# Fewer GpSimd operations for a threshold search's first points, an empty step behind them, and one scratch row for two tiles

## The chip, the cores and the metric

The kernel runs on one core of a Trainium2 chip. The core has five engines that run their own instruction queues and meet through semaphores: TensorE (PE in the profile; PEld is its weight load), VectorE (DVE), ScalarE (ACT), GpSimd (POOL) and SyncE (SP), which here only starts DMAs. The metric is the device time of one launch in microseconds; the median of several runs is compared.

## The reference

Layer 0 is a graph-attention layer over a 2708 x 2708 adjacency matrix. Layer 1 is what the change is about. It takes `X` (2708 x 512) and makes two diffusion stages:

```python
for s in range(STEPS):                       # STEPS = 2
    A = _adj_from_feats(Xa, W1, W2, W3)
    Xf = Rf @ Xf
    Xb = Rb @ Xb
    Xa = A @ Xa
    Z = Z + (Xf @ U1[s] + Xb @ U2[s] + Xa @ U3[s])
```

`_adj_from_feats` forms logits `Q W2 K^T` and takes, in every row, the smallest set of largest softmax weights that reaches 0.9 of the row's mass; the softmax is then formed over that set alone. `Rf` and `Rb` are the adjacency matrix plus identity, divided by its row sums or column sums.

## The kernel before

**Tiles and stages.** The 2708 rows are 22 tiles of 128 (the last has 20). Layer 1 works on pairs of tiles, 11 groups in each of two stages (`s` = 0 and 1). For a group, TensorE makes the logits into `p` (L517), ScalarE copies them to SBUF (L519) and takes the exponential (L549, L556), VectorE searches the threshold of each row and writes the kept weights into two rows `keep[0]` and `keep[1]`, TensorE transposes these (L1004) and multiplies them with the values `va` (L1023), and the results are mixed with the matrices `U` (L1051). The products of the adjacency matrix (L959) run between these.

**Pipelining of groups.** In one turn of the loop (index `g`), TensorE works on group `g` with kept rows found earlier, VectorE searches group `g + 1`, and ScalarE and GpSimd prepare group `g + 2`: `Logits.exp` gives a list of small steps that the attention of group `g` takes up one after the other. The list holds, for each tile, `root` (the exponential at half scale; its sum is `half`) and `full` (the exponential itself; its sum is `tot`), then `points`, then twelve looks (a Relu and a Sign pass over 2708 elements for each of three points and two tiles), then `masses`. `points` is GpSimd work: from `tot` and `half` it guesses a threshold, makes three points around it (`ABOUT`), and writes their fourth powers and the negatives `nth`, which are the biases of the looks. `masses` combines what the looks counted; the search of that group begins from it.

**Order.** TensorE, ScalarE, VectorE and SyncE run under `tc.manual_schedule`: their instructions are queued in the order in which the program states them. GpSimd's order is chosen by the framework's planner. `paced(steps, n)` takes the next `n` steps from a list. In `attended` there are twelve turns `n` (six column groups for each of two tiles): each transposes the rows for the next turn (the copy to SBUF is ScalarE's L1008, tile `at`), takes steps from the list beginning at `n` = 3, and then multiplies. In stage 0 it takes two steps at `n` = 3 to 8 and one from 9 on; in stage 1 one at 3 to 5 and two from 6 on. `mixed` takes one step at each of up to six places (the first three of four row blocks of `U1` and of `U2`). `others` holds adjacency products and, in every second group of stage 0, eight steps `scaled`: ScalarE scales a finished product (L965, tile `xe`, two buffers), GpSimd stores it (L966), and VectorE splits it into two parts (L181, L182). These groups are called split groups below, and the other ones plain groups.

**Beginning of a stage.** At `g` = -1 the program takes `5 + G * NA` = 11 steps from the list of group 1 (four exponentials, `points`, six looks), and the rest at the top of the next turn, behind the logits of group 2: `paced(looks, len(looks))`.

**The search.** `search` makes interpolation rounds (L624 sums what lies above a threshold), then `late()` queues the attention of the group before, and then `finish` runs: for each tile it writes the elements below the threshold (L800) and takes the eight largest (`MAX8`, L802), once in stage 0 and twice in stage 1; then `kept_from` (L725) or `kept_ranked` (L730 to L733) writes the kept row of each tile. `keep` has two buffers, so the row that `finish` writes for tile `i` is the row of the group before that TensorE transposes. The four buffers of `p` hold two groups: the logits of group `g + 2` go where those of group `g` lay, once the search of group `g` has ended (L884 is the branch at its end).

Of the kernel before, what the change touches and what calls it, by code (L numbers as in the profile page):

```python
# [9 lines left out]
F32 = mybir.dt.float32  # L10
# [5 lines left out]
OP = mybir.AluOpType  # L16
# [8 lines left out]
P = 128  # L25
# [6 lines left out]
X_LO = math.exp(-4.0)  # L32
# [4 lines left out]
GUESS = ((0.715, -0.82, 0.4), (0.711, -0.798, 0.392))  # L37
ABOUT = (0.88, 1.0, 1.12)
# [15 lines left out]
def kernel(  # L54
# [19 lines left out]
    nc = tc.nc  # L74
# [3 lines left out]
    STEPS = u1.shape[0]  # L78
# [12 lines left out]
    G = 2  # L91
# [4 lines left out]
    const = ctx.enter_context(tc.tile_pool(name="const", bufs=1))  # L96
# [105 lines left out]
    with ExitStack() as l0:  # L202
# [13 lines left out]
        with tc.tile_pool(name="l0w", bufs=1) as wp, tc.tile_pool(name="l0p", bufs=2) as pp, \  # L216
# [44 lines left out]
            for t in range(NT):  # L261
                pr = rows[t]
# [52 lines left out]
        small = l0.enter_context(tc.tile_pool(name="l0small", bufs=3))  # L315
# [82 lines left out]
        for ci, tiles in enumerate(tchunks):  # L398
# [4 lines left out]
            for t in range(NT):  # L403
                pr = rows[t]
# [16 lines left out]
            for grp, r_b in zip(hgroups, r_bs):  # L421
                po = [ps_o.tile([P, 512], F32, name="po")[:DV] for _ in grp]
                for t in range(NT):
                    pr = rows[t]
# [29 lines left out]
    for r, c0, c1 in [(P, 0, NFULL), (rows[-1], NFULL, NT)]:  # L454
        if c0 == c1:
            continue
        s = (slice(0, r), slice(c0, c1))
# [11 lines left out]
    powers = const.tile([P, STEPS, 2, G], F32, name="powers")  # L469
    for s in range(STEPS):  # L470
        for i in range(2):
            nc.vector.memset(powers[:, s, i], GUESS[s][i])
    weights = const.tile([P, G + 1], F32, name="weights")
    for i in range(G + 1):
        nc.vector.memset(weights[:, i:i + 1], float(1 << i))
    NA = len(ABOUT)
# [11 lines left out]
    class Logits:  # L488
# [33 lines left out]
        def exp(self, looks=True):  # L522


            _, small, _ = self.pools
            gp = nc.gpsimd
            grp = self.grp
            self.tot = small.tile([P, G], F32, name="tot")
            self.half = small.tile([P, G], F32, name="half")

            self.pts = small.tile([P, NA, 3, G], F32, name="pts")
            self.th = small.tile([P, NA, G], F32, name="th_a")
            self.thr, self.top, self.cap = (small.tile([P, G], F32, name=n) for n in ("thr", "top", "cap"))
            self.nth = small.tile([P, NA, G], F32, name="nth", bufs=1)
            self.above = small.tile([P, NA, G], F32, name="above", bufs=1)
            self.signs = small.tile([P, NA, G], F32, name="signs", bufs=1)
            self.ragged = any(rows[t] < P for t in grp) or len(grp) < G
            if self.ragged:
                for x in (self.tot, self.half, self.above, self.signs, self.pts):
                    nc.gpsimd.memset(x, 1.0)  # L540
            nmx = small.tile([P, 2, G], F32, name="nmx1")
            for i, t in enumerate(self.grp):
                pr = rows[t]
                nc.vector.tensor_reduce(nmx[:pr, 0, i:i + 1], self.p[i][:pr], axis=AX.X, op=OP.max, negate=True)  # L544

            def over(i, func, **kw):
                pr = rows[self.grp[i]]
                junk = small.tile([P, N], U8, name="junk_a", bufs=1)
                nc.scalar.activation(junk[:pr], self.p[i][:pr], func, **kw)  # L549

            def root(i, pr):
                nc.scalar.mul(nmx[:pr, 1, i:i + 1], nmx[:pr, 0, i:i + 1], 0.5)
                over(i, AF.Exp, scale=0.5, bias=nmx[:pr, 1, i:i + 1], accum_out=self.half[:pr, i:i + 1])

            def full(i, pr):
                nc.scalar.activation(self.p[i][:pr], self.p[i][:pr], AF.Exp, bias=nmx[:pr, 0, i:i + 1],  # L556
                                     accum_out=self.tot[:pr, i:i + 1])

            def points():
                x0 = small.tile([P, 2, G], F32, name="x0")  # L560
                gp.tensor_tensor(x0[:, 0], self.tot, powers[:, self.s, 0], op=OP.pow)
                gp.tensor_tensor(x0[:, 1], self.half, powers[:, self.s, 1], op=OP.pow)
                gp.tensor_tensor(x0[:, 0], x0[:, 0], x0[:, 1], op=OP.mult)
                gp.tensor_scalar(x0[:, 0], x0[:, 0], math.exp(GUESS[self.s][2]), X_LO * 1.5, op0=OP.mult, op1=OP.max)
                for j, m in enumerate(ABOUT):
                    gp.tensor_scalar(self.pts[:, j, 0], x0[:, 0], m, 0.9995, op0=OP.mult, op1=OP.min)
                gp.tensor_tensor(self.th, self.pts[:, :, 0], self.pts[:, :, 0], op=OP.mult)
                gp.tensor_tensor(self.th, self.th, self.th, op=OP.mult)
                gp.tensor_scalar(self.nth, self.th, -1.0, None, op0=OP.mult)  # L569
                gp.tensor_scalar(self.thr, self.tot, P_NUC, None, op0=OP.mult)  # L570
                gp.tensor_scalar(self.top, self.tot, 1.0 + CURVE, None, op0=OP.mult)
                gp.tensor_scalar(self.cap, self.tot, CAP, None, op0=OP.mult)

            def masses():
                gp.tensor_scalar(self.signs, self.signs, 0.5, 0.5 * N, op0=OP.mult, op1=OP.add)
                gp.tensor_tensor(self.signs, self.signs, self.th, op=OP.mult)
                gp.tensor_tensor(self.pts[:, :, 2], self.signs, self.above, op=OP.add)

            steps = []
            for i, t in enumerate(self.grp):  # L580
                steps += [lambda a=(i, rows[t]): root(*a), lambda a=(i, rows[t]): full(*a)]
            steps.append(points)
            if looks:
                for i, t in enumerate(self.grp):
                    for j in range(NA):
                        for func, to in ((AF.Relu, self.above), (AF.Sign, self.signs)):
                            def look(i=i, j=j, pr=rows[t], func=func, to=to):
                                over(i, func, bias=self.nth[:pr, j, i:i + 1], accum_out=to[:pr, j, i:i + 1])
                            steps.append(look)
                steps.append(masses)  # L590
            return steps

    def search(lg, looked, early, late):
# [4 lines left out]
        v = nc.vector  # L598
# [4 lines left out]
        keep = [wide.tile([P, N], F32, name="keep") for _ in tiles]  # L603
# [189 lines left out]
        def finish(go):  # L793


            for i, pr in tiles:
                t, m = th[:pr, i:i + 1], kept[:pr, 1, i:i + 1]
                for e in range(0, nx, 8):
                    vs, ss = vn[:pr, i, e:e + 8], sn[:pr, i, e:e + 8]
                    v.scalar_tensor_tensor(keep[i][:pr], ps_[i][:pr], t, ps_[i][:pr], op0=OP.is_lt, op1=OP.mult,  # L800
                                           accum_out=left[:pr, i:i + 1] if e else None)
                    v.max(vs, keep[i][:pr])  # L802
                    if e:
                        m = left[:pr, i:i + 1]
                        v.tensor_tensor(m, tot[:pr, i:i + 1], m, op=OP.subtract)
                    v.tensor_tensor_scan(ss, vs, vs, m, OP.add, OP.bypass)
                    t = vn[:pr, i, e + 7:e + 8]
# [58 lines left out]
        def branch(go):  # L866
# [17 lines left out]
            for arm in tc.Switch({DVE: what}, (1 << G) + 1):  # L884
                if 0 < arm < 1 << G:
                    ties([x for x in tiles if arm >> x[0] & 1])
                elif arm == 1 << G and go == 0:
                    rounds(MORE_ROUNDS)
                    choose()
                    finish(1)  # L890
                elif arm == 1 << G and go == 1:
                    v.copy_predicated(th, short, vn[:, :, nx - 1])
                    v.copy_predicated(kept[:, 1], short, den)
                    finish(2)
                elif arm == 1 << G:
                    bisect()

        late()
        finish(0)
        rden = small.tile([P, G], F32, name="rden1")  # L900
        v.reciprocal(rden, den)
        return keep, rden

    for s in range(STEPS):
        last = s == STEPS - 1
        with ExitStack() as st:
# [6 lines left out]
            small = st.enter_context(tc.tile_pool(name=f"s{s}small", bufs=2))  # L913
# [225 lines left out]
            with tc.manual_schedule(engines={PE, ACT, DVE, SP}):  # L1139
# [4 lines left out]
                steps = lg[0].exp(looks=False)  # L1144
# [4 lines left out]
                half = []  # L1149
# [90 lines left out]
```

## Time and profile before

| What | us |
|---|---|
| Median of 3 runs | 3777.57 (3777.3 to 3778.19) |
| The profiled execution, its own time | 3774.21 |
| Its span from first to last instruction | 3772.1 |
| TensorE busy | 3383.3 (90%) |
| VectorE busy | 2611.1 (69%) |
| ScalarE busy | 1540.1 (41%) |
| GpSimd busy | 838.2 (22%) |
| Mean granted TensorE clock (share of full) | 0.956 |

Layer 0 takes the span up to about 1065 us; stage 0 runs from there to about 2340 us, stage 1 from there to the end. A row of the timeline gives the start, the duration, engine and line, operation, tiles written and read, their shapes, and in brackets how long the engine had been idle and what ended the idle time. A row of the waits gives who waited for whom, the total, the number of waits and the longest. A row of the windows gives the stretch, its length, then for each engine the busy time and (number of instructions), the granted clock, the DMA share and GB/s. Times are positions in the span.

### The profile page before, as it was taken

How to read it: one execution, taken by the hardware profiler on the slowest of the kernel's cores; microseconds unless marked ns; L12 is line 12 of the kernel's file. 1: busy time of each engine (PE TensorE's matmuls, PEld its weight loads, DVE VectorE, ACT ScalarE, POOL GpSimd, SP SyncE). 2: the span in 40 equal slices, each digit the busy share in tenths (PEclk: the TensorE clock that was granted, in tenths of full speed). 3: DMA queues.
4: the chain of work that ended last, by engine and by line, in shares of the span. 5: the costliest groups of instructions: out<-in, count | busy, mean ns of one | idle time of the engine just before them, and what ended most of it. 6: DMA issues, size and time to landing. Idle time of an engine off the chain costs nothing. (4 is left out here: it accounts for less than half of the span.)

```text
span 3772.1 us, 35425 instructions
## 1 busy us (share of the span) xinstructions
PE 3383.3 (90%) x11143; PEld 1760.6 (47%) x11143; DVE 2611.1 (69%) x4814; ACT 1540.1 (41%) x2334; POOL 838.2 (22%) x1187
## 2 busy tenths in 40 slices
PE   8999999999855898989898998668999999999988
PEld 4433333333533455545454453435555665556443
DVE  4588888989946526474554641967779798777992
ACT  2343202111025565546566621335544556445511
POOL 4115151423331121121212020302121211212101
PEclk9999999999977999999999998989999999999989
DMA  3476424233154554454545352845556665567552
GB/s 115 159 255 219 155 78 140 85 99 114 44 167 143 193 197 158 154 184 146 195 146 206 114 176 83 302 130 206 187 202 225 229 209 192 197 212 243 184 192 88
DMA packets 276457, 634.07 MB, mean 168 GB/s; under 512 B 37209, under 2 KB 70441, under 8 KB 273243
## 3 DMA queue, kind: packets, MB, share of 16 engines
q1 hardware_dynamic: 249183, 540.99, 43.3%
q0 software_dynamic: 27024, 90.30, 6.3%
q8 instruction: 89, 1.46, 0.2%
q14 instruction: 161, 1.32, 0.1%
HBM read 509.07 MB, written 122.10 MB: 167 GB/s over the span
## 5 line engine op out<-in xcount | busy, mean ns | idle before, releaser
L1023 PE MATMUL a<-va,at 128*128 128x512 f32 (+2 forms) x1936 | 898.0, 603 | 58.0 <-ACT at L1008 57.9
L959 PE MATMUL q<-hl,s_r 128*128 128x512 f32 x2904 | 821.8, 429 | 67.2 <-DMA s_r<-s_d 65.7
L429 PE MATMUL po<-e,fw 128*65 128x512 f32 (+4 forms) x2112 | 840.4, 553 | 30.0 <-DVE e L427 22.2
L427 DVE SCALAR_TENSOR_TENSOR e<-r_b,kk,a_c 128x512 f32<-128x512 f32 (+4 forms) x1056 | 752.3, 741 | 68.8 <-PE po L429 18.2
L959 PEld LDWEIGHTS q<-hl,s_r 128*128 128x128 f32 x2904 | 545.8, 190 | 312.4 <-issue 147.5
L549 ACT ACTIVATE junk_a<-p,nth 128x2708 uint8<-128x2708 f32 (+1 forms) x240 | 613.0, 2554 | 93.2 <-POOL nth L569 89.6
L429 PEld LDWEIGHTS po<-e,fw 128*65 128x65 f32 (+1 forms) x2112 | 286.5, 140 | 544.2 <-issue 269.1
L1023 PEld LDWEIGHTS a<-va,at 128*128 128x128 f32 (+2 forms) x1936 | 339.6, 188 | 428.2 <-issue 347.2
L1051 PE MATMUL a<-u_k,v_t 128*128 128x512 f32 (+1 forms) x1056 | 490.8, 601 | 20.9 <-ACT xa L1031 15.1
L624 DVE SCALAR_TENSOR_TENSOR junk<-p,th 128x2708 bf16<-128x2708 f32 (+1 forms) x132 | 402.2, 3047 | 4.0
L1008 ACT COPY at<-t 128x512 f32<-128x512 f32 (+3 forms) x308 | 139.8, 476 | 439.4 <-PE t L1004 439.2
L1051 PEld LDWEIGHTS a<-u_k,v_t 128*128 128x128 f32 (+1 forms) x1056 | 188.6, 186 | 239.6 <-issue 187.0
L517 PE MATMUL t<-keys,q_t 128*128 128x452 f32 x528 | 167.9, 444 | 117.0 <-ACT p L519 95.0
L800 DVE SCALAR_TENSOR_TENSOR keep<-p,th 128x2708 f32<-128x2708 f32 (+1 forms) x44 | 133.4, 3033 | 132.4 <-PE t L1004 131.1
L181 DVE TENSOR_SCALAR split_hl<-xe 128x512 int32<-128x512 int32 (+1 forms) x44 | 19.0, 432 | 275.6 <-ACT xe L965 232.6
L802 DVE MAX8 vn<-keep 128x8 f32<-128x2708 f32 (+1 forms) x66 | 196.8, 2981 | 2.3
L519 ACT COPY p<-t 128x452 f32<-128x452 f32 (+2 forms) x264 | 132.7, 539 | 149.8 <-DVEq L884 78.9
L517 PEld LDWEIGHTS t<-keys,q_t 128*128 128x128 f32 x528 | 91.8, 211 | 188.7 <-ACT p L519 149.5
L411 ACT ACTIVATE s_c<-a_c 128x512 fp32r<-128x512 f32 (+3 forms) x132 | 76.2, 577 | 248.3 <-DMA a_c<-in_adj_t_dram 123.2
L1004 PE MATMUL t<-ident,keep 128*128 128x128 f32 (+1 forms) x968 | 146.4, 273 | 21.9 <-DVE keep L752 16.5
L1004 PEld LDWEIGHTS t<-ident,keep 128*128 128x128 f32 (+1 forms) x968 | 114.5, 138 | 105.1 <-issue 76.9
L544 DVE TENSOR_REDUCE nmx<-p 128x1 f32<-128x2708 f32 (+1 forms) x44 | 129.2, 2966 | 40.3 <-ACT p L519 40.1
(294 smaller groups left out, 3105.1 us busy)
## 6 DMA issues: line engine op xcount, KB each, us to landing
s_r<-s_d SPq DMA_DIRECT2D x330, 256.0 KB
hl<-vhl_d SPq DMA_DIRECT2D x132, 512.0 KB
u_k<-in_L_gnn_U_dram SPq DMA_DIRECT2D x264, 256.0 KB
hl<-fhl_d SPq DMA_DIRECT2D x132, 512.0 KB
hl<-bhl_d SPq DMA_DIRECT2D x132, 512.0 KB
arow<-in_adj_dram SPq DMA_DIRECT2D x21, 1354.0 KB
s_d<-s_c SPq DMA_DIRECT2D x88, 256.0 KB
a_c<-in_adj_t_dram SPq DMA_DIRECT2D x84, 256.0 KB
```

The lines of the kernel that those rows point to most:

```text
L427: nc.vector.scalar_tensor_tensor(e[:pr, :cw], r_b[:pr, i, :cw], kk[:pr, t, hd:hd + 1], a_c[t][:pr, :cw], op0=OP.max, op1=OP.mult)
L429: nc.tensor.matmul(po[i][:, :cw], lhsT=fw[:pr, t, hd, :], rhs=e[:pr, :cw], start=(t == 0), stop=(t == NT - 1))
L517: nc.tensor.matmul(pl[:, :c1 - c0], lhsT=q[:, i], rhs=self.keys[:, c0:c1], start=(i == 0), stop=(i == 1))
L549: nc.scalar.activation(junk[:pr], self.p[i][:pr], func, **kw)
L624: v.scalar_tensor_tensor(junk_b[:pr], ps_[i][:pr], th, ps_[i][:pr], op0=OP.is_ge, op1=OP.mult, accum_out=dst)
L800: v.scalar_tensor_tensor(keep[i][:pr], ps_[i][:pr], t, ps_[i][:pr], op0=OP.is_lt, op1=OP.mult, accum_out=left[:pr, i:i + 1] if e else None)
L802: v.max(vs, keep[i][:pr])
L959: nc.tensor.matmul(half[j], lhsT=s_r[:, j * P:(j + 1) * P], rhs=hl[:, h], start=(c == 0 and h == 0), stop=(c == NT - 1 and h == 1))
L1004: nc.tensor.transpose(pt[:rows[c], j, :pr], keep[i][:pr, cols[c]], ident[:pr, :pr])
L1008: nc.scalar.copy(at[:r, j0:j1, :pr], pt[:r, j0:j1, :pr])
L1023: nc.tensor.matmul(pa[:pr], lhsT=at[:rows[c], j, :pr], rhs=va[:rows[c], c, :], start=(c == 0), stop=(c == NT - 1))
L1051: nc.tensor.matmul(pz[i][:rows[t]], lhsT=v_t[i][:, k, :rows[t]], rhs=u_k, start=(n == 0 and k == 0), stop=(n == 2 and k == KD - 1))
```

## The change

Four things change.

- `tot` and `half` become two halves of one tile `sums`, and one power operation over 4 elements a partition replaces two over 2.
- The factor `exp(GUESS[s][2])` and the three factors `ABOUT` are multiplied into a constant table `about`, which six small VectorE memsets fill once. One multiplication and one clamp over 6 elements replace one scaling with a lower clamp and three scalings with an upper clamp. The lower clamp is now set after the factors, at 1.2 in place of 1.5 times `X_LO`. `points` has ten GpSimd operations in place of thirteen.
- An empty step stands in the list between `points` and the first look, so every look and `masses` are taken one place later.
- `finish` writes the rows below the threshold of both tiles into `keep[0]`; `keep[1]` is first written by `kept_from` or `kept_ranked` of tile 1.

```diff
+    about = const.tile([P, STEPS, len(ABOUT), G], F32, name="about")
+    for s in range(STEPS):
+        for j, m in enumerate(ABOUT):
+            nc.vector.memset(about[:, s, j], m * math.exp(GUESS[s][2]))
...
-            self.tot = small.tile([P, G], F32, name="tot")
-            self.half = small.tile([P, G], F32, name="half")
+            self.sums = small.tile([P, 2, G], F32, name="sums")
+            self.tot, self.half = self.sums[:, 0], self.sums[:, 1]
...
-                gp.tensor_tensor(x0[:, 0], self.tot, powers[:, self.s, 0], op=OP.pow)
-                gp.tensor_tensor(x0[:, 1], self.half, powers[:, self.s, 1], op=OP.pow)
+                gp.tensor_tensor(x0, self.sums, powers[:, self.s], op=OP.pow)
                 gp.tensor_tensor(x0[:, 0], x0[:, 0], x0[:, 1], op=OP.mult)
-                gp.tensor_scalar(x0[:, 0], x0[:, 0], math.exp(GUESS[self.s][2]), X_LO * 1.5, op0=OP.mult, op1=OP.max)
-                for j, m in enumerate(ABOUT):
-                    gp.tensor_scalar(self.pts[:, j, 0], x0[:, 0], m, 0.9995, op0=OP.mult, op1=OP.min)
-                gp.tensor_tensor(self.th, self.pts[:, :, 0], self.pts[:, :, 0], op=OP.mult)
+                x = self.pts[:, :, 0]
+                gp.tensor_tensor(x, x0[:, 0].unsqueeze(1).to_broadcast([P, NA, G]), about[:, self.s], op=OP.mult)
+                gp.tensor_scalar(x, x, X_LO * 1.2, 0.9995, op0=OP.max, op1=OP.min)
+                gp.tensor_tensor(self.th, x, x, op=OP.mult)
...
             steps.append(points)
             if looks:
+
+                steps.append(lambda: None)
...
-                    v.scalar_tensor_tensor(keep[i][:pr], ps_[i][:pr], t, ps_[i][:pr], op0=OP.is_lt, op1=OP.mult,
+                    v.scalar_tensor_tensor(keep[0][:pr], ps_[i][:pr], t, ps_[i][:pr], op0=OP.is_lt, op1=OP.mult,
                                            accum_out=left[:pr, i:i + 1] if e else None)
-                    v.max(vs, keep[i][:pr])
+                    v.max(vs, keep[0][:pr])
```

More of the change, by code (lines that the diff above doesn't have):

```diff
@@ L538, in exp @@
             if self.ragged:
-                for x in (self.tot, self.half, self.above, self.signs, self.pts):
+                for x in (self.sums, self.above, self.signs, self.pts):
                     nc.gpsimd.memset(x, 1.0)
```

## The prediction

> **What bounds the kernel now.** I read the page first, where TensorE is busy for 3383.3 us of 3772.1 us, and then the windows over single groups: one split and one plain group of stage 0, one of stage 1.
>
> ```profile
> 1332.26:1442.95 110.69, 97.98 (x332) 54.67 (x332) 49.08 (x87) 64.22 (x83) 30.39 (x54) 0.97 0.59 208
> 1442.95:1542.45 99.50, 98.12 (x333) 55.16 (x333) 58.09 (x147) 60.13 (x75) 8.39 (x21) 0.98 0.37 120
> 2777.45:2894.13 116.68, 114.05 (x404) 68.95 (x404) 107.80 (x187) 61.70 (x75) 21.00 (x28) 1.00 0.62 210
> ```
>
> The columns after the length are PE, PEld, DVE, ACT, POOL. In a plain group and in stage 1 TensorE lacks 1.4 and 2.6 us of being full; in a split group it lacks 12.7 us. ScalarE and GpSimd are far from full everywhere, so what matters is which of their waits TensorE feels. The waits:
>
> ```profile
> ACT junk_a L549 <- POOL nth L569: 89.6, 19, 9.8
> DVE keep L800 <- PE t L1004: 131.1, 8, 28.3
> PE t L517 <- ACT p L519: 95.0, 75, 15.0
> PE a L1023 <- ACT at L1008: 57.9, 27, 15.7
> PE q L959 <- DMA s_r<-s_d: 65.7, 39, 17.1
> ```
>
> The first two are what the change aims at; the last three are TensorE's own. The timeline of a split group shows how they are joined.
>
> ```profile
> 1371.75 0.80 POOL L566 TENSOR_SCALAR pts<-x 128x2 f32<-128x2 f32 x3
> 1373.19 0.25 POOL L569 TENSOR_SCALAR nth<-th_a 128x6 f32<-128x6 f32 x1
> 1373.47 2.55 ACT L549 ACTIVATE junk_a<-p,nth 128x2708 uint8<-128x2708 f32 x1 [3.58 <-POOL nth L569]
> ...
> 1388.27 0.59 ACT L1008 COPY at<-t 128x512 f32<-128x512 f32 x1 [0.18 <-PE t L1004]
> ...
> 1410.30 0.69 ACT L965 ACTIVATE xe<-q,cinv 128x512 f32<-128x512 f32 x1 [1.37 <-DMA xfb_d<-xe]
> ...
> 1414.85 3.03 DVE L800 SCALAR_TENSOR_TENSOR keep<-p,th 128x2708 f32<-128x2708 f32 x1
> ...
> 1442.95 7.51 PE L517 MATMUL t<-keys,q_t 128*128 128x452 f32 x20 [7.37 <-ACT p L519]
> ```
>
> ScalarE waits 3.58 us for `nth`, but at 1388.27 it has already caught up and waits for TensorE. TensorE's 7.37 us come from VectorE's search, which ends late because `finish` stands behind the last split, which stands behind the last `xe`. Three more split groups have the same gap (10.97, 8.30, 8.93 us).
>
> **What the Trainium skill says.** "PSUM — Partial Sum Buffer", Engine vs sequencer instructions: the queues of ScalarE, VectorE and GpSimd are strict FIFO. The trace agrees: no copy passes the look that waits 3.58 us. "SBUF — State Buffer", Who interferes with whom: a VectorE instruction with two SBUF inputs contends with a GpSimd instruction that reads SBUF. The trace agrees, and here it decides a step: during VectorE's L624 pair (2560.29 to 2566.4) two operations that otherwise take 0.22 us took 2.5 and 3.0, and a third did so in the next pair.
>
> ```profile
> 2560.92 2.50 POOL L570 TENSOR_SCALAR thr<-tot 128x2 f32<-128x2 f32 x1
> 2563.49 3.00 POOL L571 TENSOR_SCALAR top<-tot 128x2 f32<-128x2 f32 x1
> ...
> 2569.58 2.81 POOL L569 TENSOR_SCALAR nth<-th_a 128x6 f32<-128x6 f32 x1
> ```
>
> **Part 1, the GpSimd chain.** From the end of the second `full` to `nth` the undisturbed chain takes 3.97 us (1369.50 to 1373.47). Removed: L564 and three L566, from 1371.44 to 1372.63, 1.19 us. Added: a multiplication (0.20, as L567) and a clamp (0.23, as L564), with 0.08 between operations 0.59. The power over 4 elements is not in the trace; over 1 element L140 takes 0.589, over 2 L561 takes 0.70, so I take 0.92, and the ends are 0.70 and 1.0 if cost were flat or a little steeper. Net 1.19 - 0.59 - 0.22 = 0.4 us shorter (0.3 to 0.6). The six memsets take 0.06 us each, as L636's, and lie where VectorE waits 21.01 us for stage 0's first logits (1099.76): nothing, and 0.4 us without that cover.
>
> Where is this on the path? At the start of each stage VectorE itself waits for the points of group 0 (11.53 us at 1118.10, 1.25 us at 2390.82), and TensorE then waits for that search (15.00 and 12.33 us). So -0.4 us in each stage.
>
> **Part 2, the empty step.** In the turns, the copy for the next turn now stands before the first look. A look is 2.55 + 0.19 us, 2.7 with the gap.
>
> Split and plain groups: between the copy at 1388.27 and `xa` of the second tile stand five looks before and five after, since all move one place; what ScalarE gains before 1388.27 (3.58 of wait, one look) turns into waiting for TensorE. The last `xe`, the splits and the end of the search don't move. The look that goes past the end now stands before the copy of the transposed `xa`: 1416.48 becomes about 1419.2, ending at 1420.3. The product that reads it is the third of the mixing, and starts 7 us after 1418.59, at 1425.6: hidden. In stage 1 ScalarE waits 8.75 us at that place (2749.94). `masses` comes 2.7 us later and is read 30 us later. Zero.
>
> Start of stage 0: of twelve looks six were taken early, now five; TensorE's wait for the first copy (15.74 us at 1215.56) grows by one look, +2.7. Then the copy at 1265.70 no longer stands behind the look that waited 4.37 us, which gives back TensorE's 2.07 us, and `xe` comes a look sooner, which gives back 1.28. One look is still missing: at 1273 TensorE stands +2.7 - 3.35 = -0.7.
>
> Last group of stage 0 with looks (2119 to 2147): the quad has two tiles, TensorE has less to do, and ScalarE sets the pace: gaps of 1.13, 0.62, 1.77 and 1.09 us. Alone this edit would give back some 2.9 us here. But see part 3.
>
> Start of stage 1: again one look more behind the logits, +2.7 - 0.4 (part 1). Next comes this:
>
> ```profile
> 2579.97 3.75 PE L959 MATMUL q<-hl,s_r 128*128 128x512 f32 x8 [17.09 <-DMA s_r<-s_d]
> ```
>
> SyncE's load of `s_r` is queued behind loads of `xfb_d`, whose stores GpSimd issues behind `points` (2568.88, and 2572.34 behind the blocked `nth`). All moves with the search. If `nth`, 0.4 to 0.6 us sooner, slips in ahead of VectorE's L624 at 2569.24, 3.07 us are won (-0.8 in all); if it doesn't, the store waits as before (+2.3). It ends within 0.05 us of that start by my count, so I take the middle, +0.7.
>
> **Part 3, `keep[0]` for both tiles.** In the four plain groups VectorE's L800 of tile 1 waits for the transposes of `keep[1]`:
>
> ```profile
> 1509.47 3.04 DVE L800 SCALAR_TENSOR_TENSOR keep<-p,th 128x2708 f32<-128x2708 f32 x1 [28.17 <-PE t L1004]
> ```
>
> That wait moves to `kept_from` of tile 1, past L800, MAX8 and one `kept_from` (3.04 + 2.98 + 3.03, with small operations some 10 us). The search then ends at 1520 rather than 1530, but TensorE asks for its `p` at 1541 and feels 0.73 us: the work of group `g` hides it; without that cover it would be worth 10 us. What is next late is VectorE's L544, which waits for the new `p` anyway. In split groups L800 doesn't wait; in stage 1 one group waits (12.74 us), also covered. Cost: L800 of tile 1 now runs at once, from 1481.2, beside the points (from 1481.6), and holds GpSimd up until it ends, as at 1164.47, where an operation of 0.20 us took 2.78 beside L800: about +2.2 us on `nth`, hidden in plain groups with whole quads. In the group at 2119 the same (2113.8 to 2116.8) puts `nth` at 2119.3 and takes back 2.6 of the 2.9 us.
>
> **Sum.** Stage 0: -0.4 - 0.7 - 0.3 = -1.4. Stage 1: -0.4 is contained in +0.7. In all -0.7 (-2.2 to +0.8) against the span of 3772.1, whose execution took 3774.21; the runs' median is 3.4 above that execution. Added to the median: 3776.9.
>
> **Rivals.**
>
> *ScalarE's wait is TensorE's loss in split groups (faster).* If the last `xe` came sooner by the wait and a look (3.6 + 2.7 = 6.3 us), four groups would give 25 us: 3752. For it: four gaps of 35.6 us in sum exist. Against: ScalarE waits for TensorE at 1388.27, between the two.
>
> *The pile at 2580 goes (faster).* If the planner puts the stores ahead of the rest of `points`, most of the 17.09 us go, up to 11: 3767. For: `xe` was ready at 2561.2. Against: nothing in the diff reorders it.
>
> *The later look is felt (slower).* Had the copy of `xa` been needed by the second product of the mixing, the four plain groups of stage 0 would lose a look each, 4 x 2.7 = 11: 3788; stage 1 has 8.75 us of slack. It decides when the copy ends after 1425.6, and it has 5 us to spare in a split group. Split groups would stay hidden behind VectorE's end.
>
> *The empty step does nothing by itself:* that is my forecast for the steady groups.
>
> **How the numbers follow.** Near no change 0.68, with an own range of 3773 to 3781; faster by the first two rivals or a like one 0.19; slower by the third, or by a GpSimd order that the planner makes worse, 0.13. 0.2% is 7.5 us, about what a measurement of this kernel can tell from no change. Leaving out the outer half of the rivals on both sides gives 3767 to 3783.
>
> **What would show it.** Right: L549's wait for `nth` nearly gone from the waits and ScalarE's wait for L1004 grown; L800's wait for L1004 moved to L725; TensorE's gaps of 7 to 11 us before L517 still there; 17 to 19 us before the first copy in both stages. Wrong: split gaps shrink below 5 us, or new gaps stand before L1051 in plain groups, or the 17.09 us gap changes by more than 3.

## The result and the profile after

Before had a median of 3778.19 us in 20 runs, the changed kernel 3772.72 us in 20 runs beside it. The ratio is 0.9987 with a 95% interval of 0.9981 to 0.9993: 4.9 us less, 2.6 to 7.2 us by the interval, which is a difference, but one inside the 0.2% (7.5 us) that the prediction set for "no change". Two later comparisons of the same two kernels gave 0.999 (0.9983 to 0.9997) and 0.999 (0.9982 to 0.9999). The forecast was no measurable change at 3776.9; the value lies inside its range (3767 to 3783) and 4.2 us under its point.

In the changed kernel the lines have moved: L517, L519, L549, L569, L624, L725, L800, L959, L965, L966, L1004, L1008, L1023 and L1051 of before are now L521, L523, L553, L572, L629, L730, L806, L965, L971, L972, L1010, L1014, L1029 and L1057. So L965 is ScalarE's `xe` in before and the adjacency products in the changed kernel; in the kernels of the experiments the lines lie up to six further on than in before. The profiled execution has a span of 3775.9 us. The windows over the three groups that the prediction showed (a split and a plain group of stage 0, one of stage 1; the columns after the length are PE, PEld, DVE, ACT, POOL):

```profile
1336.52:1447.15 110.63, 96.81 (x332) 53.83 (x332) 49.09 (x87) 64.43 (x83) 28.65 (x51) 0.98 0.59 210
1447.15:1546.57 99.42, 98.32 (x332) 55.43 (x332) 60.55 (x153) 60.55 (x75) 9.90 (x20) 0.98 0.36 119
2779.22:2895.84 116.62, 113.95 (x404) 68.95 (x405) 106.17 (x187) 61.91 (x75) 20.42 (x25) 1.00 0.61 210
```

All three groups are as long as before within 0.1 us (110.69, 99.50, 116.68): the inside of a steady group has no price for this change. GpSimd's busy time fell from 838.2 to 805.9 us and its instructions from 1187 to 1119, and TensorE felt none of it there.

The waits (who waited for whom: total, number, longest):

```profile
ACT at L1014 <- PE t L1010: 500.6, 179, 19.3
PE t L521 <- ACT p L523: 91.6, 76, 12.6
PE q L965 <- DMA s_r<-s_d: 65.6, 38, 17.7
ACT junk_a L553 <- POOL nth L572: 63.0, 16, 9.2
DVE keep L730 <- PE t L1010: 61.4, 4, 17.2
PE a L1029 <- ACT at L1014: 59.9, 22, 18.4
```

VectorE's wait at the row below the threshold (131.1 us in 8 waits) has turned into four waits at L730; three short ones (5.4 us) are left at L806. TensorE's own three waits moved by 3.4, 0.1 and 2.0 us in total. ScalarE's wait for `nth` only fell from 89.6 to 63.0 us. The timeline of a split group shows why the fall brought nothing:

```profile
1373.79 1.05 POOL L565 TENSOR_TENSOR x<-sums,powers 128x4 f32<-128x4 f32 x1 [30.85 <-ACT p L560]
...
1377.25 0.26 POOL L572 TENSOR_SCALAR nth<-th_a 128x6 f32<-128x6 f32 x1
1377.43 0.59 ACT L1014 COPY at<-t 128x512 f32<-128x512 f32 x1 [1.76 <-PE t L1010]
1377.91 2.56 ACT L553 ACTIVATE junk_a<-p,nth 128x2708 uint8<-128x2708 f32 x1
...
1384.98 0.59 ACT L1014 COPY at<-t 128x512 f32<-128x512 f32 x1 [1.75 <-PE t L1010]
...
1414.54 0.69 ACT L971 ACTIVATE xe<-q,cinv 128x512 f32<-128x512 f32 x1 [1.37 <-DMA xfb_d<-xe]
1419.05 3.03 DVE L806 SCALAR_TENSOR_TENSOR keep<-p,th 128x2708 f32<-128x2708 f32 x1
...
1447.15 3.24 PE L521 MATMUL t<-keys,q_t 128*128 128x452 f32 x7 [8.08 <-ACT p L523]
```

The copy now stands ahead of the first look, and the wait of 3.58 us is gone. ScalarE waits for TensorE instead, 1.76 us before this copy and 1.75 before the next. The last `xe` still waits 1.37 us for its buffer, the search still follows it, and the gap in front of the logits is 8.08 us (7.37 before). The other three are 8.22, 8.30 and 9.09 us.

**Where the time went.** Whole executions scatter by some 10 us, so the account is made by stretches between TensorE's milestones, with three traces of the changed kernel and two of before (lengths in us):

| Stretch of TensorE | Before | After | Mean change | Predicted |
|---|---|---|---|---|
| start to stage 0's first logits | 1093.9, 1095.0 | 1099.1, 1091.8, 1094.1 | +0.6 | 0 |
| to the first copy of stage 0 | 121.7, 122.2 | 124.1, 124.4, 124.5 | +2.4 | +2.3 |
| to the first split gap's end | 227.4, 227.1 | 223.9, 223.4, 222.9 | -3.9 | -3.35 |
| to the last split gap's end | 634.2, 631.6 | 630.6, 629.1, 629.5 | -3.2 | 0 |
| to the end of stage 0 (group at 2119) | 261.8, 261.4 | 260.3, 260.1, 260.1 | -1.4 | -0.3 |
| to the gap of 17 us in stage 1 | 241.0, 241.3 | 243.9, 240.2, 243.4 | +1.4 | +2.3 or -0.8 |
| steady stage 1, up to its last group | 1018.1, 1018.9 | 1016.8, 1016.9, 1017.0 | -1.6 | 0 |
| last group to the end | 174.0, 174.0 | 177.2, 177.0, 177.1 | +3.1 | 0 |

The sum is -2.6 us, -3.2 without layer 0, beside -3.8 to -4.9 us in the timed runs. The four stretches for which a change was forecast (+2.3, -3.35, -0.3 and +0.7, the middle of the two values) give -1.5 us for a forecast of -0.7; the three others of layer 1 give -1.7 us, as what is left of -3.2, -1.6 and +3.1. So the sum is near the forecast in part by luck: terms that nobody forecast, each as large as the forecast ones, nearly cancel.

### The profile page after: what moved, and what is told of

Its sections match the earlier page's. It is cut to its first block, busy times and chain, and to the rows that moved or that the text cites. A ratio compares the mean times of both kernels' runs of the same rounds, so it can differ in the third digit from the quotient of the medians.

```text
span 3775.9 us, 35382 instructions
## 1 busy us (share of the span) xinstructions
PE 3382.8 (90%) x11143; PEld 1762.6 (47%) x11143; DVE 2608.9 (69%) x4820; ACT 1543.0 (41%) x2334; POOL 805.9 (21%) x1119
## 5 line engine op out<-in xcount | busy, mean ns | idle before, releaser
L1029 PE MATMUL a<-va,at 128*128 128x512 f32 (+2 forms) x1936 | 898.0, 603 | 60.2 <-ACT at L1014 59.9
L965 PE MATMUL q<-hl,s_r 128*128 128x512 f32 x2904 | 822.5, 430 | 65.8 <-DMA s_r<-s_d 65.6
L965 PEld LDWEIGHTS q<-hl,s_r 128*128 128x128 f32 x2904 | 547.8, 191 | 309.5 <-issue 149.1
L553 ACT ACTIVATE junk_a<-p,nth 128x2708 uint8<-128x2708 f32 (+1 forms) x240 | 613.0, 2554 | 66.8 <-POOL nth L572 63.0
L1029 PEld LDWEIGHTS a<-va,at 128*128 128x128 f32 (+2 forms) x1936 | 340.0, 188 | 429.5 <-issue 346.8
L1057 PE MATMUL a<-u_k,v_t 128*128 128x512 f32 (+1 forms) x1056 | 490.3, 601 | 19.7 <-ACT xa L1037 14.6
L629 DVE SCALAR_TENSOR_TENSOR junk<-p,th 128x2708 bf16<-128x2708 f32 (+1 forms) x132 | 401.3, 3040 | 4.0
L1014 ACT COPY at<-t 128x512 f32<-128x512 f32 (+3 forms) x308 | 140.5, 478 | 500.6 <-PE t L1010 500.6
L1057 PEld LDWEIGHTS a<-u_k,v_t 128*128 128x128 f32 (+1 forms) x1056 | 188.8, 186 | 237.8 <-issue 186.0
L521 PE MATMUL t<-keys,q_t 128*128 128x452 f32 x528 | 168.2, 446 | 113.6 <-ACT p L523 91.6
L523 ACT COPY p<-t 128x452 f32<-128x452 f32 (+2 forms) x264 | 132.6, 539 | 157.8 <-DVEq L890 83.3
L521 PEld LDWEIGHTS t<-keys,q_t 128*128 128x128 f32 x528 | 92.2, 212 | 185.1 <-ACT p L523 145.7
L1010 PE MATMUL t<-ident,keep 128*128 128x128 f32 (+1 forms) x968 | 147.4, 274 | 26.5 <-DVE keep L757 18.8
L1010 PEld LDWEIGHTS t<-ident,keep 128*128 128x128 f32 (+1 forms) x968 | 115.1, 139 | 109.6 <-issue 82.2
L565 POOL TENSOR_TENSOR x<-sums,powers 128x4 f32<-128x4 f32 x22 | 49.2, 2238 | 495.3 <-ACT p L560 495.3
```

The source lines that it names most:

```text
L521: nc.tensor.matmul(pl[:, :c1 - c0], lhsT=q[:, i], rhs=self.keys[:, c0:c1], start=(i == 0), stop=(i == 1))
L523: nc.scalar.copy(p[:pr, c0:c1], pl[:pr, :c1 - c0])
L629: v.scalar_tensor_tensor(junk_b[:pr], ps_[i][:pr], th, ps_[i][:pr], op0=OP.is_ge, op1=OP.mult, accum_out=dst)
L965: nc.tensor.matmul(half[j], lhsT=s_r[:, j * P:(j + 1) * P], rhs=hl[:, h], start=(c == 0 and h == 0), stop=(c == NT - 1 and h == 1))
L1010: nc.tensor.transpose(pt[:rows[c], j, :pr], keep[i][:pr, cols[c]], ident[:pr, :pr])
L1014: nc.scalar.copy(at[:r, j0:j1, :pr], pt[:r, j0:j1, :pr])
```

## The experiments

Theory A is the prediction's account by stretches. The rivals are told in each expectation.

**The changed kernel, a second time** (no edit).

> The changed kernel once more, beside its own profile taken a second time. Theory A (the sum of the prediction, about -0.7 us, and the rest of the measured -4.9 us is drift of single executions): -1 to -5 us against the kernel before, and the position of stage 0's first logits, where the code is the same in both kernels, moves by some us from one profile to the next (1093.9 before, 1099.1 after). Theory B (the change itself moves layer 0, by where its tiles and instructions lie): the first logits stand at 1099 us again, within 1 us. Theory C (the four gaps in front of the logits of split groups shorten): the gaps are again 8.1, 8.2, 8.3 and 9.1 us and none is near 11 us; by theory A a gap of 10 to 11 us can stand at any of the four.

Measured: 3774.82 us against 3776.52, ratio 0.999 (0.9983 to 0.9997), so about -3.8 us. (Here and below the ratio with its interval counts; the plain difference of the two medians can be up to 3 us away from it.) The first logits stood at 1091.8 us: theory B, that this build has a longer layer 0, fails for this kernel. The split gaps were 7.9, 8.0, 7.1 and 9.1 us. None was near 11, so theory C isn't excluded by this run; but a gap of 10.95 to 11.03 us stood in one of these four places in one trace each of five other builds: before, the ten operations alone, the empty step alone, the changed kernel with two scratch rows and the one with six looks early, which has every part of the change. So it is put down to scatter.

The prediction left open whether `nth` slips in ahead of VectorE's search at the start of stage 1, and took the middle. This trace showed the other case. GpSimd in the first and then in the second trace of the changed kernel, with TensorE's gap of the second:

```profile
2569.59 0.66 POOL L972 DMA_DIRECT2D xfb_d<-xe  x1
2570.33 3.06 POOL L572 TENSOR_SCALAR nth<-th_a 128x6 f32<-128x6 f32 x1
2573.33 1.14 POOL L972 DMA_DIRECT2D xfb_d<-xe  x2
```

```profile
2559.46 0.66 POOL L972 DMA_DIRECT2D xfb_d<-xe  x1
2560.20 0.24 POOL L572 TENSOR_SCALAR nth<-th_a 128x6 f32<-128x6 f32 x1
2560.40 0.59 POOL L972 DMA_DIRECT2D xfb_d<-xe  x1
...
2569.03 3.52 PE L965 MATMUL q<-hl,s_r 128*128 128x512 f32 x8 [14.71 <-DMA s_r<-s_d]
```

In the first, VectorE's L629 had started at 2570.22, just ahead of `nth`, which took 3.06 us; in the second, L629 started at 2560.20, together with `nth`, which took 0.24. The store behind it comes 2.8 us sooner, and the gap in front of L965 is 14.71 us in place of 17.72. A third trace also gave 0.24 and 14.69. The chances of the two cases are not even: in the seven traces with the ten operations, the two with the looks moved ahead aside, `nth` took 0.24 us in six (in those two it took 2.46); in all four traces with the thirteen operations it started 0.34 to 0.53 us behind VectorE's operation and took 2.61 to 2.81 us. The shorter chain thus mostly wins this race.

**One part alone.** First the ten operations of GpSimd, without the empty step and with two scratch rows (the edit is shown against the changed kernel; here and below the `v.max` behind the row reads the same row):

```diff
-                steps.append(lambda: None)
-                    v.scalar_tensor_tensor(keep[0][:pr], ...
+                    v.scalar_tensor_tensor(keep[i][:pr], ...
```

> The ten operations of GpSimd in place of thirteen, without the empty step and with two scratch rows. Theory A: the chain is 0.23 us shorter (3.72 for 3.95), felt only where VectorE waits for the points of group 0 at the start of each stage: -0.5 us, and not outside -2 to +1. Rival (the chain is what ScalarE and then TensorE wait for in every group): 19 waits shorter by 0.23 us in both tiles' first look, -4 to -5 us, which would be the whole measured gain.

Measured: 3775.32 us, ratio 0.9994 (0.9988 to 1.0001), about -2.3 us. The undisturbed chain is 0.23 us shorter, as said. Its trace has the start of stage 0 and the group at 2119 within 0.6 us of before, as theory A has it. The timing is just outside the -2 to +1 by its middle, with zero inside the interval: it doesn't decide between the two. The trace speaks against the rival: if every group gained, the steady stretches would be shorter, and they take 632.0 and 1020.3 us (634.2 and 631.6, 1018.1 and 1018.9 before). What is shorter is the start of stage 1, 239.3 us for 241.0 and 241.3, with `nth` in 0.24 us.

The empty step alone:

```diff
             if looks:
+                steps.append(lambda: None)
```

> The kernel before with the empty step alone. Theory A: start of stage 0 -0.7 us (+2.7 and -3.4), the last group of stage 0 with looks -2.9 us, start of stage 1 +2.7 us: -0.9 us in all (-4 to +2). Gaps in front of the logits of split groups stay between 7 and 11 us. Rival (ScalarE's wait for the points is TensorE's loss in the split groups): these gaps shrink by up to 6.3 us each, -25 us.

Measured: 3777.01 us, ratio 0.9994 (0.9988 to 1.0001), about -2.3 us. The split gaps were 10.95, 7.87, 8.15 and 7.44 us: the rival of -25 us is out. Its trace has the gain at the group at 2119 (shown below), but the start of stage 1 took 245.9 us there, 4.8 more than before where 2.7 were said, and layer 1 as a whole 2680.1 us (2678.2 and 2676.5 before). So this one trace doesn't give the -2.3 us of the timing.

The scratch row alone:

```diff
-                    v.scalar_tensor_tensor(keep[i][:pr], ps_[i][:pr], t, ...
+                    v.scalar_tensor_tensor(keep[0][:pr], ps_[i][:pr], t, ...
-                    v.max(vs, keep[i][:pr])
+                    v.max(vs, keep[0][:pr])
```

> The kernel before with the scratch row of the first tile alone. The look now stands directly behind the points on ScalarE, so a delay of the points is a delay of the copies behind it. Theory A: the write of tile 1 runs at once, beside the points, and holds them up by 2 to 3 us in the plain groups of stage 0; ScalarE then waits 6 us instead of 4 there, which TensorE feels in the last group with looks (+2.2 us) and by up to 1 us in the four plain groups: 0 to +4 us. Rival (the wait of the write of tile 1 for the transposes was on the path): the four plain groups of stage 0 each lose up to 2.5 us: -5 us or more.

Measured: 3781.58 us, ratio 1.001 (1.0001 to 1.0018), about +3.8 us: slower, at the upper end of theory A, and the rival is out. In its trace the place that was named costs 2.5 us; 2.0 more stand in the steady stage 1, without an explanation, and 3.3 at the very end, where every build but before has them, whatever was changed. So the trace doesn't show the 3.8 us of the timing to be the scratch row's alone. VectorE, GpSimd, ScalarE and TensorE in the group at 2119 of this kernel:

```profile
2109.97 3.03 DVE L800 SCALAR_TENSOR_TENSOR keep<-p,th 128x2708 f32<-128x2708 f32 x1
2110.11 2.96 POOL L571 TENSOR_SCALAR top<-tot 128x2 f32<-128x2 f32 x1
...
2115.74 2.55 ACT L549 ACTIVATE junk_a<-p,nth 128x2708 uint8<-128x2708 f32 x1 [6.31 <-POOL nth L569]
...
2118.86 0.57 ACT L1008 COPY at<-t 128x512 f32<-128x512 f32 x1
...
2119.48 5.14 PE L1023 MATMUL a<-va,at 128*128 128x512 f32 x8 [3.84 <-ACT at L1008]
```

The five rows make one chain. The write of the second tile runs at once, 0.14 us ahead of a GpSimd operation that takes 2.96 us in place of 0.22. The Trainium skill, "SBUF — State Buffer", Who interferes with whom, says that the order of issue decides who blocks. This trace agrees, 0.14 us being enough to lose 2.7, and so does the blocked `nth` above, 0.11 us behind; where both start in the same 0.01 us, the trace can't tell which was first. ScalarE waits 6.31 us (3.58 in before), its copy comes late, and TensorE stands 3.84 us where it stood 1.13.

The same place in before, and then in the kernel with the empty step alone:

```profile
2120.72 3.70 PE L1023 MATMUL a<-va,at 128*128 128x512 f32 x8 [1.13 <-ACT at L1008]
...
2132.11 3.70 PE L1023 MATMUL a<-va,at 128*128 128x512 f32 x8 [0.62 <-ACT at L1008]
...
2137.80 3.70 PE L1023 MATMUL a<-va,at 128*128 128x512 f32 x8 [1.77 <-ACT at L1008]
```

```profile
2121.07 3.60 PE L1025 MATMUL a<-va,at 128*128 128x512 f32 x8
...
2131.57 3.60 PE L1025 MATMUL a<-va,at 128*128 128x512 f32 x8
...
2135.82 3.70 PE L1025 MATMUL a<-va,at 128*128 128x512 f32 x8 [0.44 <-ACT at L1010]
```

The gaps of 1.13 and 0.62 us are gone and the one of 1.77 is down to 0.44. From the last split gap to the end of stage 0 this kernel takes 258.1 us (261.4 and 261.8 before: -3.5), the scratch row alone 264.1 (+2.5), and both together 260.1 to 260.3.

**Before, a second time** (no edit).

> The kernel before, unchanged, for a second trace of it. Time: the same, within 2 us. Trace, theory A (the account by stretches, with one switch in it: whether nth at the start of stage 1 runs ahead of or behind VectorE's L624): stretches measured from TensorE's milestones repeat within 1 us where no switch lies in them: first logits to first copy of stage 0 121.7 us, first copy to the first split gap's end 227.4, the stretch from the last split gap to the end of stage 0 261.8 with gaps of 1.1, 0.6, 1.8 and 1.1 us in the group at 2119. Where the profile of before was itself off by more (634.2 us from the first to the last split gap, 174.0 us from the last group of stage 1 on, both of which other versions gave as 629 to 632 and 177 us), the second trace should give 630 to 632 and 177 us.

Measured: 3778.51 us, ratio 1.0003 (0.9995 to 1.0012). The stretches repeat, and the one with the split gaps came down to 631.6, so some 2.7 us of its 634.2 were scatter. One expectation failed: from the last group to the end it again took 174.0 us, where every other build, whatever was changed, takes 177 to 178. It lies in VectorE's small operations on the flag of the last search. VectorE and TensorE in before, and then in the changed kernel:

```profile
3687.77 0.67 DVE L876 COPY flag<-flag_t 1x3 f32<-1x3 f32 x4
...
3690.45 1.06 PE L1004 MATMUL t<-ident,keep 128*128 128x128 f32 x8 [1.50 <-DVEq L884]
```

```profile
3688.43 2.07 DVE L882 COPY flag<-flag_t 1x3 f32<-1x3 f32 x4
...
3692.52 1.94 PE L1010 MATMUL t<-ident,keep 128*128 128x128 f32 x8 [4.71 <-DVEq L890]
```

The last transposes wait for the end of this search. Both traces of before have 0.67 us for the four copies, and TensorE's gap is 1.4 to 1.5 us. The eleven traces of the other builds have 0.99 to 2.82 us for them and a gap of 4.0 to 4.9; where it is 0.99 (twice), the operation L875, a little ahead, takes 1.19 or 1.24 us in place of 0.15. The code there is the same in all; what delays it was not found.

**Fewer operations and the empty step, two scratch rows.**

```diff
-                    v.scalar_tensor_tensor(keep[0][:pr], ...
+                    v.scalar_tensor_tensor(keep[i][:pr], ...
```

> The changed kernel with two scratch rows again: fewer operations of GpSimd and the empty step, without the first tile's row for both. Theory A: the group at 2119 has no gap but the last one of 1.1 us (3.5 us less than before, about 2 us less than the changed kernel), the plain groups are as before, all else as in the changed kernel: -2 us against the changed kernel, -5 to -7 us against before. Rival (the three changes need each other; the scratch row's gain shows once the empty step stands behind the points): slower than the changed kernel, -1 to -3 us against before.

Measured: 3777.74 us against 3778.66, ratio 1.0 (0.9991 to 1.0008): the expectation of -5 to -7 us missed. Its trace does what was said: the group at 2119 has lost its gaps down to 0.27 and 1.09 us, and that stretch takes 258.0 us, 2.1 less than in the changed kernel; from the first logits to the end it takes 2672.7 us (2678.2 and 2676.5 before). But the first logits stand at 1101.3 us. The same kernel again:

> Fewer operations of GpSimd and the empty step, two scratch rows, a second time: its first measurement was 0.9 us below before where the account of its trace says about 5. Theory A (its layer 0, which stood 7 us later in that one trace, is drift of single executions): the first logits come between 1092 and 1100 us, layer 1 is again 2672 to 2674 us long, and the time is -4 to -6 us. Rival D (layer 0 of this build is longer, though it has the same instructions in the same order): first logits at 1100 us or later again, and the time within 2 us of before.

Measured: 3775.72 us against 3777.42, ratio 0.9996 (0.9988 to 1.0004), and the first logits at 1100.5 us. Rival D is favoured: this build's layer 0 was 6 to 7 us longer than that of before in both traces, though all five engines have the same instructions there in the same order, but for six memsets of 0.20 us together at the very start. Two traces don't show it, as the changed kernel's own three traces lie 7.3 us apart. The second trace's layer 1 was 2677.0 us, with a 10.97 us split gap in it, so the mean of the two is about that of the changed kernel. The timings of -0.9 and -1.7 us by the medians also fit the rival of the first expectation (-1 to -3 us), and only the stretch of the group at 2119 (258.0 and 258.5 us) speaks for theory A. In that place the scratch row costs 2 us; in the whole time this isn't seen.

**Six looks early again.** The changed kernel, with one more step at the start of a stage:

```diff
-                        paced(fills, 5 + G * NA)
+                        paced(fills, 6 + G * NA)
```

> The changed kernel with twelve steps taken early at the start of each stage in place of eleven, so that again six looks are early and six stand behind the logits of group 2. Theory A: the gap in front of the first copy of each stage goes from 18.4 back to 15.7 us and what the empty step gave back at the start of stage 0 stays: -5.4 us against the changed kernel, -9 to -10 us against before. Rival (the looks there are covered by other waits right behind, such as that for s_r in stage 1): the gaps behind grow by what the first one loses, and the time is that of the changed kernel within 2 us.

Measured: 3767.84 us against 3778.66, ratio 0.9971 (0.996 to 0.9981), about -11 us against before: theory A. TensorE's first gap of stage 0 in before, in the changed kernel and in this one:

```profile
1215.56 6.72 PE L1023 MATMUL a<-va,at 128*128 128x512 f32 x8 [15.74 <-ACT at L1008]
```

```profile
1223.28 5.42 PE L1029 MATMUL a<-va,at 128*128 128x512 f32 x8 [18.41 <-ACT at L1014]
```

```profile
1219.43 5.29 PE L1029 MATMUL a<-va,at 128*128 128x512 f32 x8 [15.75 <-ACT at L1014]
```

The gap is 15.75 us in both stages, and the stretch to the first split gap kept its 223.9 us. The rival (the gaps behind grow) is out: the two starts are 2.5 and 4.1 us shorter than the mean of the changed kernel.

**The looks moved ahead.** All of them and `masses` in stage 1, nine in stage 0:

```diff
-                        paced(fills, 5 + G * NA)
+                        paced(fills, len(fills) if last else 9 + G * NA)
```

> The changed kernel with the looks moved ahead as far as ScalarE is free: four more looks early in stage 0 (three behind the logits), all of them and masses early in stage 1. Theory A: stage 0 -8 to -10.8 us (three or four of the looks in the 18.4 us gap; ScalarE waits 8.1 us for the logits there, which three looks fit into), stage 1 -18.7 us (the whole gap; ScalarE waits 44.8 us there): -27 us against the changed kernel, about 3746. Rival (the search of group 0 and the load of s_r, not ScalarE's looks, hold the start of stage 1): its first gap goes, the gap of 14.7 to 17.7 us in front of L965 grows by as much, and only stage 0's share of -8 us is left, about 3765.

Measured: 3749.1 us against 3778.66, ratio 0.992 (0.9906 to 0.9933), about -30 us against before. TensorE at the start of stage 1, first in the changed kernel and then in this one:

```profile
2504.89 7.98 PE L521 MATMUL t<-keys,q_t 128*128 128x452 f32 x20 [12.53 <-ACT p L523]
2532.55 6.14 PE L1029 MATMUL a<-va,at 128*128 128x512 f32 x8 [18.41 <-ACT at L1014]
2581.93 0.76 PE L965 MATMUL q<-hl,s_r 128*128 128x512 f32 x1 [17.72 <-DMA s_r<-s_d]
```

```profile
2498.64 6.78 PE L521 MATMUL t<-keys,q_t 128*128 128x452 f32 x16 [9.85 <-ACT p L523]
...
2508.27 3.70 PE L1029 MATMUL a<-va,at 128*128 128x512 f32 x8 [0.24 <-ACT at L1014]
2554.42 3.75 PE L965 MATMUL q<-hl,s_r 128*128 128x512 f32 x8 [16.93 <-DMA s_r<-s_d]
```

The gap of 18.41 us is 0.24, and the one for `s_r` didn't take the gain: it is 16.93, between the two values seen. In stage 0 the first gap is 7.71 us. From the first logits of stage 0 to the end this kernel takes 2648.5 us, 25.6 less than the mean of the changed kernel's three traces (27 said).

**The same with two scratch rows.**

```diff
-                    v.scalar_tensor_tensor(keep[0][:pr], ...
+                    v.scalar_tensor_tensor(keep[i][:pr], ...
```

> The kernel with looks and masses moved ahead, and two scratch rows in place of the first tile's for both. Theory A: the gap of 1.8 us in the group at 2119 goes (with the first tile's row it stands there), about -2 us against the front-loaded kernel: 3747, -31 us against before. Rival (the one scratch row makes the whole gain of the change): +3 to +4 us against it, 3752 to 3753.

Measured: 3744.05 us against 3777.42, ratio 0.9914 (0.9901 to 0.9928): the fastest version, about 32 us below before. The group at 2119 again lost its 1.8 us gap, and its stretch is 258.1 us for 260.1. The rival that the scratch row makes the gain is out here. The medians of the two front-loaded kernels come from different runs and overlap, so their difference in time isn't settled.

**The changed kernel, a third time** (no edit).

> The changed kernel a third time, for its trace. Theory A: layer 1 from the first logits to the end lasts 2671 or 2674 to 2677 us, the first if nth at the start of stage 1 runs in 0.24 us ahead of L629, the second if it is held up to 3.06 us by it; the time is -3 to -5 us. Rival D (layer 0 differs by build): first logits near one of the two places seen, 1091.8 and 1099.1 us, which by then were seen for one build.

Measured: 3771.34 us against 3777.42, ratio 0.999 (0.9982 to 0.9999); layer 1 2674.5 us, with `nth` in 0.24 us; the first logits at 1094.1 us. The length is that of the blocked case although `nth` ran free: the load of the next `s_r` came as early as in the second trace (14.69 us gap), but TensorE came to the logits of group 2 2.7 us later than in that trace, counted from the end of stage 0. For this kernel layer 0 has thus been seen from 1091.8 to 1099.1 us.

## Why the prediction was right, point by point

**Split and plain groups: zero.** Right. The wait for `nth` went from every split group, and ScalarE waits for TensorE in its place; the gaps in front of the logits stayed between 7.09 and 9.10 us in the changed kernel's three traces. The -3.2 us of that stretch weren't predicted: 2.7 us separate the two traces of before alone, so most of it is scatter, and what is left isn't explained.

**Start of stage 0: +2.7 - 0.4, then -3.35.** Right: +2.4 and -3.9. The first gap grew from 15.74 to 18.41 us, and six early looks took exactly that back.

**The group at 2119: -2.9 and +2.6.** The two mechanisms were right, and each was shown alone in the trace: -3.5 us with the empty step, +2.5 with the scratch row. Together they make -1.4, not -0.3: the row takes back 2.0 of 3.5, which fits a copy that now stands ahead of the delayed look (argued, not tested apart).

**Start of stage 1: +2.3 or -0.8.** Both ends occurred in one kernel: +2.8, -0.9, +2.3 us in three traces. The race of `nth` with VectorE was named rightly, but it doesn't set the length alone: `nth` ran free in the second and in the third trace. Taking the middle was luck; as six of seven traces with the ten operations have `nth` free, -0.8 was the likelier case, and the mean is still +1.4. (The upper end of the range in the prediction's sum comes to +0.9, not +0.8.)

**The chain: 0.4 us shorter, power 0.92 us.** Mis-sized: where VectorE doesn't hold it up (9 of 22 in the first trace), the power over 4 elements took 1.04 to 1.07 us, past the upper bound of 1.0, and the chain is 0.23 us shorter. By the prediction's own sum this is 0.2 us less gained in each stage. The six memsets were also put in the wrong place: they don't run while VectorE waits for stage 0's logits but at the start of the launch, where they are too short to matter.

```profile
1.00 0.20 DVE L476 MEMSET about<- 128x2 f32 x6
```

**L549's wait for `nth` "nearly gone".** Wrong: 63.0 of 89.6 us are left, 42.6 of 49.7 in stage 1 and 20.4 of 39.9 in stage 0. In stage 1 one step is taken in turns 3 to 5 and two from turn 6, so `points` was already the last of its turn and a copy already stood ahead of the first look; the empty step changes nothing there. The wait, 2.8 to 6.0 us in most groups of stage 1, stays, and as the group of stage 1 above is no longer than before, TensorE doesn't feel it. In stage 0 the scratch row keeps part of the wait: with two rows 11.4 us are left there. The step that failed was reading the order of stage 0 into both stages, and leaving the delay that the prediction itself gave `nth` by the scratch row (2.2 us in plain groups) out of this sign.

**What was left out.** In the last group of stage 1 that has looks, TensorE's gaps of 1.55 and 0.83 us (at 3526 and 3543 in before) are gone, the counterpart of the group at 2119, which the prediction didn't look for; the next gap, for the kept row, grows from 16.53 to 18.84 us and takes most of it back. At the end 3.1 us come from the late copies of VectorE, in every build but before.

**Rivals.** The 25 us of the split groups and the felt product that reads `xa` didn't occur. The gap in front of the load at 2580 shrank by 2 to 3 us when `nth` ran free, not by 11.

What stays open: layer 0, whose end lies up to 9.7 us apart between traces, 7.3 us between those of one build, and with it which part of the 4 us is the change. The traces come from several chips, but the chip alone doesn't decide it: on one chip four builds stood 6.9 us apart, and one build stood 0.8 us apart on two. The account of layer 1 gives 3.2 of the 4 us, and about half of these lie in stretches where no mechanism was found.

## What to carry to other kernels

A wait on an engine that catches up before the next thing that others need from it was worth nothing here, however often it stands in the list; the idle time just in front of the bound engine's gaps is where to look. Here the large gaps stood at the starts of the stages, where ScalarE had 45 us free ahead of the logits in stage 1 and 8 us in stage 0, and yet did its looks behind them: moving them cost one line and gave 26 us more, some six times what the change gave. When edits work against each other in one place, price each alone there: -3.5 and +2.5 us are easy to see in one group's timeline and hard to see in 3778.

## What the runs showed of the hardware that was not expected

- GpSimd's power operation on 128 partitions takes 1.04 us over 4 elements where nothing holds it up, after 0.589 over 1 and 0.70 to 0.72 over 2; one over 4 still beats two over 2 by 0.36 us or more in GpSimd's own time, though on the chain it stands for one of them and is 0.34 us longer.
- A GpSimd operation of 0.22 us that starts 0.14 us after a VectorE operation with two inputs in SBUF takes 2.96 us, and one that starts 0.11 us after it 3.06; one that starts within 0.01 us of it takes 0.24 (three traces). A change of 0.1 us upstream thus moves the next store by 2.8 us.
- Four copies of three elements on VectorE took 0.67 us in one build and up to 2.82 in the others, with equal code; and layer 0 ended 6 to 7 us later than before in both traces of one build, with equal instructions in equal order but for 0.20 us of memsets. Differences of a few us between builds can lie where nothing was changed.
